# Low-rank k and q of four octets at a time on eight TensorE tiles, and experts by slots of two octets

## The chip, the cores and the metric

The kernel runs on one core of a Trainium2 chip. The metric is the device time of one execution in microseconds (us), lower is better. The engines are named as in the profile: PE (TensorE), with PEld its weight loads, DVE (VectorE), ACT (ScalarE), POOL (GpSimd), and SP (SyncE), whose queue issues all DMAs here.

## The reference

Two layers on x of 4 images, 64 channels, 256 x 256 pixels, float32. Both add their result to x and begin with a group norm (32 groups).

```
layer 0, per image, x the normalised input:
  h  = gelu(conv3x3(x, c1) + c1_b)
  xa, k = split(c2 * h + c2_b)                    # 64 + 64 channels, 1x1
  xs = gelu(conv over columns(conv over rows(xa)))  # 3 taps each, per channel
  weights = softmax(mean over pixels(xs) @ gate.T); the best two of three experts are kept
  out = xs + sum over experts e of  mask_e * w3_e (  (w2_e k + b2_e) * (w1_e xs + b1_e) )
  layer 0 = x_in + proj(out)
layer 1:
  h = relu(batchnorm(conv3x3(x, quantised w1)))
  h = batchnorm(conv3x3(h, quantised w2));   layer 1 = x_in + relu(h + x)
```

The three experts have 2, 4 and 8 ranks, 14 in all. The change is in the experts: `low = (w2 k + b2) * (w1 xs + b1)` has 14 (padded to 16) rows per pixel, and its product with w3 and proj is added to layer 0's result once the image's gate is known.

## The kernel before

An image is 128 pairs of rows. 128 partitions hold 64 channels of two rows; a *group* is 2 pairs (512 elements of a partition), an *octet* 4 pairs (8 rows), a *chunk* 8 pairs. Each image has 32 octets and 16 chunks.

A dictionary `plan` holds (step, order) for every call, and all calls are written out in that order (`at(step, order, call)`). In the first stage, the *front*, one step is one octet: 4 x 32 = 128 steps (`CONV1` = 128). For octet n of image b at step g = 32 b + n, PE's order in a step is

- order 1 and 7: `front_conv_a`, `front_conv_b` with products (1, 2) of octet n, the 3x3 convolution on 64x64 tiles into one of two PSUM banks `ps_c`; order 3 and 8 of the next step do products (0, 3);
- 7.5 and 8.5: `front_butterfly` (ACT and DVE) and `front_h`: two gelu activations that make h of one octet from its `ps_c` bank and so free it;
- step g + 3, order 4 and 9: `front_taps_a`, `front_taps_b` (`ps_a`, one bank), order 11 `front_taps_h`: t on ACT, two additions and the ends on DVE, then xs by gelu on ACT;
- step g + 4, order 6: `front_proj` (`ps_p`), added by DVE, stored to `t1_d`;
- order 2: the experts of image b - 1 (`out_octets`), order 3.5 the statistics of image b + 1;
- order 10: `front_k` and `front_q`, each for two octets j = 0 to 15: k at step 2j + 4, q at step 2j + 5.

Thus every step of the front has either a k or a q behind its last taps group. `front_v` (order 9 and 9.5) makes the convolution's inputs on POOL in `v_ring`. `divide` (order 5) puts a tiny POOL operation, the tick, between two uses of a bank.

`front_k` multiplies h with a weight `wk` whose other 64 rows are zero, on tiles of 128 rows by 32 columns: four groups of 512 to four strips of 32 partitions, ACT copies them to `k`. `front_q` does the same from xs, DVE adds a bias and multiplies by k into `low`, which goes to DRAM (`low_d`). Bank `p` (one buffer) is used by k, q, proj, the experts and all small matmuls in turn.

`plan_out` runs an image behind: `low_load` and `out_load` bring `ranks` and y back, `out_octets` makes two matmuls from 32 rows (`ps_o`) for one octet, and DVE adds each group to y (L746) and takes its statistics (L747). PE, SP, DVE and POOL keep the written order; ACT keeps it from step 124 on, and before that the scheduler orders it.

After step 128 the second stage (`conv1`, two steps per octet) runs layer 1's first convolution of all images, while the last octets of the front are done at half the pace (`tail`), and the experts of image 3 are spread over it. `leave` takes its result from PSUM: ACT makes `m`, DVE adds. `conv1_prepare` and `conv1_add` put sums of pixels in the buffers of t and xs. Then conv2 and a last stage follow, which the change doesn't touch in substance.

Of the kernel before, what the change touches and what calls it, by code (L numbers as in the profile page):

```python
# [17 lines left out]
B, C, H, W = 4, 64, 256, 256  # L18
P = 128


# [24 lines left out]
GP = 2  # L46
GF = GP * W
# [15 lines left out]
def conv_preact_kernel(ctx: ExitStack, tc: tile.TileContext, io, col128, colset, col64):  # L63
# [23 lines left out]

    low_d = [dram.tile([P, NG // 4, GF], F32, name=f"low_d{b}") for b in range(B)]
    y_d = [dram.tile([P, NPAIR, W], F32, name=f"y_d{b}") for b in range(B)]
# [99 lines left out]
    def weights():  # L189

        mset = flat(chunk_x("mset"))[:, 0 : io["mset"].shape[1]]
        m64_t = work.tile([P, 2, GF], F32, tag="xs", name="m64", bufs=3)
        m64 = flat(m64_t)[0:C, 0 : io["m64"].shape[1]]
# [129 lines left out]

    def leave(h, ps, ps_m, n, name, pool, tag, w, bias):

        m = pool.tile([P, 4 * HW], F32, tag=tag, name=f"m_{name}", bufs=2)[:, 0 : n * HW]
        nc.scalar.activation(m, by_two(ps_m)[:, 0, 0 : n * HW], AF.Identity, bias=bias, scale=w_scale[w])  # L327
        nc.vector.scalar_tensor_tensor(  # L328
            h.rearrange("p a (b e) -> p e (a b)", e=2),
            by_two(ps)[:, :, 0 : n * HW],  # L330
            w_scale[w],
            m.unsqueeze(1).to_broadcast([P, 2, n * HW]),
            ALU.mult,
            ALU.add,
        )
# [45 lines left out]
    def stats_group(b, g):  # L381
        if g == 0:
            st_x[b] = stat.tile([P, NG, 6], F32, tag="st_x", name=f"st_x{b}")
        t = x_in[b, g // CG]
        i = g % CG * GP
        nc.vector.bn_stats(st_x[b][:, g, :], t[:, i : i + GP, :])  # L386
# [216 lines left out]
    def front_taps_h(b, n):  # L603

        ps = open_a.pop((b, n)).rearrange("p a b c -> p (a b) c")
        t = work.tile([P, 2 * GP, W], F32, tag="t", name=f"t_{b}_{n}", bufs=1)
        nc.scalar.activation(flat(t), flat(ps), AF.Identity, bias=tap_bias, scale=sh[:, 1:2])  # L607
        nc.vector.scalar_tensor_tensor(  # L608
            t[:, :, 1:W], ps[:, :, 0 : W - 1], sh[:, 0:1], t[:, :, 1:W], ALU.mult, ALU.add
        )  # L610
        nc.vector.scalar_tensor_tensor(  # L611
            t[:, :, 0 : W - 1], ps[:, :, 1:W], sh[:, 2:3], t[:, :, 0 : W - 1], ALU.mult, ALU.add
        )
        nc.vector.tensor_tensor(  # L614
            t[:, :, 0 : W : W - 1],
            t[:, :, 0 : W : W - 1],
            ends.unsqueeze(1).to_broadcast([P, 2 * GP, 2]),
            ALU.subtract,
        )
        for at_n, slot, row in ((0, 0, 0), (NOCT - 1, 1, GP + 1)):  # L620
            if n == at_n:
                edge = t[0:C, row, :]
                nc.vector.tensor_tensor(edge, edge, outer[0:C, slot, :], ALU.subtract)
        xss[b, n] = work.tile([P, 2, GF], F32, tag="xs", name=f"xs_{b}_{n}", bufs=3)
        nc.scalar.activation(flat(xss[b, n]), flat(t), AF.Gelu, accum_out=pooled[b][:, n : n + 1])  # L625

    def front_k(b, j):

        ps = flat(bank("p", f"ps_k_{b}_{j}")[:, 0])
        for t in range(2):  # L630
            for q in range(4):
                nc.tensor.matmul(  # L632
                    ps[32 * q : 32 * q + 32],
                    wk[:, q % 2, t, :],
                    flat(hs[b, 2 * j + q // 2, t]),
                    start=(t == 0),
                    stop=(t == 1),
                )
        k_sb[b, j] = work.tile([P, GF], F32, tag="k", name=f"k_{b}_{j}")
        nc.scalar.activation(k_sb[b, j], ps, AF.Identity, bias=k_bias)  # L640

# [22 lines left out]
    def front_q(b, j):  # L664

        ps = flat(bank("p", f"ps_q_{b}_{j}")[:, 0])
        for q in range(4):
            x = xss[b, 2 * j + q // 2][:, q % 2]
            nc.tensor.matmul(ps[32 * q : 32 * q + 32], c128("e_w1"), x, start=True, stop=True)  # L669
        for n in (2 * j, 2 * j + 1):  # L670
            del xss[b, n]
        low = work.tile([P, GF], F32, tag="low", name=f"low_{b}_{j}")
        nc.vector.scalar_tensor_tensor(low, ps, c128("e_b1"), k_sb.pop((b, j)), ALU.add, ALU.mult)
        nc.sync.dma_start(low_d[b][:, j, :], low)
# [4 lines left out]
    def gate(b):  # L679
# [26 lines left out]
        for e, (i, j) in enumerate(((3, 4), (0, 5), (1, 2))):  # L706
# [3 lines left out]

        pick = stat.tile([P, 3, 3], F32, tag="pick", name=f"pick_{b}")
        of = c128("of").rearrange("p (i e) -> p i e", e=3)
        nc.vector.tensor_tensor(pick[:, 0:2, :], keep.unsqueeze(1).to_broadcast([P, 2, 3]), of, ALU.mult)
        nc.vector.tensor_tensor(pick[:, 2, :], keep, pb3, ALU.mult)
        row = stat.tile([P, 3], F32, tag="row", name=f"row_{b}")
        nc.vector.tensor_reduce(row, pick, AX.X, ALU.add)
        wm[b] = lstat.tile([P, 2, C], F32, tag="wm", name=f"wm_{b}", bufs=B)
        nc.vector.tensor_tensor(
            wm[b], row[:, 0:2].unsqueeze(2).to_broadcast([P, 2, C]), pw3.unsqueeze(1).to_broadcast([P, 2, C]), ALU.mult
        )  # L720
        out_bias[b] = stat.tile([P, 1], F32, tag="ob", name=f"ob_{b}", bufs=B)
        nc.vector.tensor_tensor(out_bias[b], row[:, 2:3], c128("proj_b"), ALU.add)

# [4 lines left out]
    def low_load(b, k):  # L728
        lows[b, k] = work.tile([P, GF], F32, tag="ranks", name=f"ranks_{b}_{k}", bufs=3)
        nc.sync.dma_start(lows[b, k], low_d[b][:, k, :])  # L730

    def out_octets(b, k, octets):


        if k == 0 and 0 in octets:
            st_y[b] = stat.tile([P, NG, 6], F32, tag="st_y", name=f"st_y{b}")
        ps = bank("p", f"ps_o_{b}_{k}_{octets[0]}")
        ranks = lows[b, k]
        for n, i in enumerate(octets):
            for g in range(2):  # L740
                rows = slice(64 * i + 32 * g, 64 * i + 32 * g + 32)
                nc.tensor.matmul(flat(ps[:, 2 * n + g]), flat(wm[b][rows]), ranks[rows], start=True, stop=True)  # L742
        for n, i in enumerate(octets):
            for g in range(2):
                y = ys[b, k][:, 4 * i + g : 4 * i + g + 3 : 2, :]
                nc.vector.scalar_tensor_tensor(y, ps[:, 2 * n + g], out_bias[b], y, ALU.add, ALU.add)  # L746
                nc.vector.bn_stats(st_y[b][:, 4 * k + 2 * i + g, :], y)  # L747
        if 1 in octets:
            y = ys.pop((b, k))
            del lows[b, k]  # L750
            for half in range(2):
                for g in range(2):
                    nc.sync.dma_start(
                        y_v[b][half, g][:, k * CG : (k + 1) * CG],
                        y[half * C : half * C + C, g::2],
                    )
# [30 lines left out]
    def conv1_add(b, k):  # L787
        sums_in[b, k] = add_pixels(y_in[b, k], f"1_{b}_{k}", [(work, "xs", 3)] * 2, [P, 2, GF])

    def conv1_prepare(b, k):  # L790

        places = (work, "t", 1), (work, "xs", 3)
        sums_in[b, k] = add_pixels(y_in[b, k], f"1_{b}_{k}", places, [P, 2, GF])
# [17 lines left out]
    def conv1_b(b, d):  # L811
# [12 lines left out]
        h = h_out[b][:, i : i + 2 * GP, :]  # L824
        leave(h, ps, ps_m, 2 * GP, f"1_{b}_{d}", work, "low", "w1", c128("b1"))
        for g in range(2):
# [9 lines left out]
    def conv1_end(b):  # L836
# [6 lines left out]
        convolve_sum(ps_m, "w1", sums[(NCH - 1) % 2], CPAIR, 1, (0,))  # L843
        leave(h, ps, ps_m, 1, f"1_{b}_end", work, "low", "w1", c128("b1"))
        nc.vector.bn_stats(st_h[b][C:P, NG, :], h[C:P, 0, :])
# [36 lines left out]
    def plan_front(b):  # L882
# [6 lines left out]
        for n in range(NOCT):  # L889
# [18 lines left out]
            at(place(g + 3), 11, front_taps_h, b, n)  # L908
        for j in range(NG // 4):
            at(place(t + 2 * j + 4), 10, front_k, b, j)  # L910
            at(place(t + 2 * j + 5), 10, front_q, b, j)
        e = place(t + NOCT + 3)
# [14 lines left out]
    def plan_out(b, steps, order, end):  # L927

        for k in range(NCH):
            for call in (low_load, out_load):  # L930
                at(steps[2 * k - 3] if k > 1 else steps[0] - 2, order + 0.2, call, b, k)
            for i in range(2):
                at(steps[2 * k + i], order, out_octets, b, k, (i,))
        at_each(end, out_end(b))
# [135 lines left out]
    def conv2_out(d, h, ps, ps_m):  # L1070
        b, k = chunks[d // 2]
        n = d % NOCT
        leave(h, ps, ps_m, 2 * GP, f"2_{d}", halves_pool, "m", "w2", c128("b2"))
        for g in range(2):
# [89 lines left out]
def _layout(a):  # L1164
# [43 lines left out]

    of = np.zeros((2, 2, 2, 2, 16, 3), f)
    for half, group in np.ndindex(2, 2):  # L1210
        of[half, :, group, half ^ group, np.arange(NLOW), expert] = 1.0
    chan = np.arange(P) % C
# [8 lines left out]
        "gate": twice(l0["gate_w"].T[:, [0, 1, 2, 0, 0, 1, 1, 2, 2]]),  # L1221
        "of": of.transpose(1, 2, 3, 4, 0, 5).reshape(P, 6),
        "sh": twice(l0["sh_w"].reshape(C, 3)),
# [37 lines left out]
```

## Time and profile before

| | us |
|---|---|
| median of 3 runs | 3368.22 (3367.95 to 3368.89) |
| profiled execution | 3364.82 |
| its span | 3363.0 |
| PE busy | 2730.7 (81%) |
| DVE busy | 2707.6 (81%) |
| ACT busy | 1668.5 (50%) |
| POOL busy | 1610.5 (48%) |
| front | about 68 to 1510 us |
| conv1 | about 1520 to 2270 us, with the experts of image 3 up to about 2070 |
| conv2, then the last stage | about 2285 to 2890 us, then to the end |

The span lies between the first and the last instruction of the profiled execution, its time contains a little more. "L441" is a line of the kernel; L441 records all quarter matmuls, so its groups are told apart by their tiles (`ps_c`, `ps_a`, `ps_p`). One fp32 matmul of the program is two MATMUL instructions in the profile. In an instruction row the idle time before it and its releaser stand in brackets.

### The profile page before, as it was taken

Reading aid. Unit: us, or ns where it says so; the run is one execution under the profiler, and the core shown is the slowest. Engines: PE = TensorE matmul, PEld = TensorE weight load, DVE = VectorE, ACT = ScalarE, POOL = GpSimd, SP = SyncE. Lnnn points to the kernel's source line nnn. Section 1 sums busy time; section 2 is a strip of 40 time slices with the busy share of each in tenths; the row PEclk is TensorE's granted clock in tenths of the full one; section 3 lists DMA queues with packets and bytes.
Section 4 is the critical chain, followed back from the end, with each engine's and each line's share of the span. In section 5 each row is a group of like instructions: output and inputs, shape, how many; then the busy total and the mean of one; then the engine's idle time right before and its main releaser. Section 6 shows DMA issues by size and latency. Waiting matters only on the chain.

```text
span 3363.0 us, 60903 instructions
## 1 busy us (share of the span) xinstructions
PE 2730.7 (81%) x24832; PEld 1758.7 (52%) x24832; DVE 2707.6 (81%) x2970; ACT 1668.5 (50%) x1831; POOL 1610.5 (48%) x1833
## 2 busy tenths in 40 slices
PE   2999999999999999997899999998999999300000
PEld 1555545555555555544667677777877878200000
DVE  7676588878888777775899998998999999866666
ACT  0344444344444443444556666767777777322222
POOL 2444544443444444444678777666777777100000
PEclk9999999999999999998999999999999999655555
DMA  8665688879887767774789887664666664599999
GB/s 299 171 184 131 160 262 267 249 199 275 259 262 208 212 192 199 209 202 139 244 276 298 300 286 239 222 249 182 238 232 237 239 239 165 207 412 412 412 412 389
DMA packets 365671, 838.28 MB, mean 249 GB/s; under 512 B 23312, under 2 KB 285968, under 8 KB 302672
## 3 DMA queue, kind: packets, MB, share of 16 engines
q1 hardware_dynamic: 365392, 834.40, 75.1%
q8 instruction: 195, 3.19, 0.4%
q14 instruction: 84, 0.69, 0.1%
HBM read 493.00 MB, written 341.31 MB: 248 GB/s over the span
## 4 chain that ended last, share of the span: by engine, by line
PE 71%; DVE 11%; DMA 11%; ACT 2%; SPq 2%; issue 2%; POOL 1%; ACTq 0%; DVEq 0%; POOLq 0%
PE ps_h L304 25%; PE ps_c L441 19%; DMA y_end<-y_d 10%; PE ps_a L441 9%; PE ps_h2m L304 3%; PE ps_k L632 3%; PE ps_o L742 3%; PE ps_p L441 3%; PE ps_hm L304 3%; PE ps_q L669 2%; DVE half L348 2%; DVE h L328 1%; DVE st_x L386 1%; SPq L1148 1%; ACT v L1139 1%
## 5 line engine op out<-in xcount | busy, mean ns | idle before, releaser
L304 PE MATMUL ps_h<-half,w_q 128*128 128x512 f32 x4096 | 1036.3, 405 | 28.6 <-DVE h L328 22.3
L304 PEld LDWEIGHTS ps_h<-half,w_q 128*128 128x128 f32 x4096 | 780.8, 192 | 260.4 <-issue 29.2
L484 POOL TENSOR_TENSOR v_ring<-x 128x256 f32<-128x256 f32 x1024 | 596.0, 614 | 157.4 <-PE ps_c L441 111.3
L364 POOL TENSOR_TENSOR sum<-s,sum 128x640 fp32r<-128x640 f32 (+1 forms) x256 | 556.6, 2194 | 193.8 <-ACT sum L362 188.2
L328 DVE SCALAR_TENSOR_TENSOR h<-ps_h,scale_w,m 128x1024 f32<-128x1024 f32 x256 | 326.9, 1277 | 92.6 <-ACT m L327 92.4
L441 PE MATMUL ps_c<-v_ring,u 64*64 64x256 f32 (+1 forms) x6472 | 389.2, 371 | 13.2 <-POOL v_ring L484 9.2
L441 PE MATMUL ps_c<-v_ring,c1s 64*64 64x256 f32 (+1 forms) x6472 | 386.1, 368 | 0.5 <-DVE ps_c L552 0.5
L441 PE MATMUL ps_a<-h,av 64*64 64x512 f32 (+1 forms) x3568 | 382.3, 530 | 1.7 <-DVE t L611 1.6
L441 PEld LDWEIGHTS ps_c<-v_ring,u 64*64 64x64 f32 x6472 | 254.0, 133 | 242.4 <-issue 77.5
L434 POOL MEMSET tick<- 128x1 f32 x132 | 13.0, 98 | 697.0 <-PE ps_a L441 686.8
L441 PEld LDWEIGHTS ps_c<-v_ring,c1s 64*64 64x64 f32 x6472 | 261.8, 133 | 134.4 <-issue 38.7
L550 ACT ACTIVATE m<-ps_c 128x512 f32<-128x512 f32 x128 | 76.6, 598 | 474.6 <-PE ps_c L441 467.6
L625 ACT ACTIVATE xs<-t 128x1024 f32<-128x1024 f32 x128 | 135.3, 1057 | 326.1 <-DVE t L614 293.5
L1139 ACT ACTIVATE v<-y_end,shift,gn 128x2048 f32<-128x2048 f32 x64 | 133.8, 2092 | 320.6 <-DMA y_end<-y_d 313.8
L1140 DVE SCALAR_TENSOR_TENSOR h<-h,ss,v 128x2048 f32<-128x2048 f32 x64 | 150.2, 2351 | 159.8 <-DMA h<-h_d 94.3
L348 DVE TENSOR_TENSOR half<-h,half 128x1280 fp32r<-128x1280 f32 (+1 forms) x128 | 254.4, 2029 | 7.7 <-ACT half L346 7.7
L656 DVE TENSOR_TENSOR x<-ps_p,x 128x1024 f32<-128x1024 f32 x128 | 156.3, 1221 | 121.2 <-PE ps_p L441 100.7
L608 DVE SCALAR_TENSOR_TENSOR t<-ps_a,m,t 128x1020 f32<-128x1020 f32 x128 | 163.6, 1278 | 93.8 <-ACT t L607 93.8
L441 PEld LDWEIGHTS ps_a<-h,av 64*64 64x64 f32 x3568 | 163.8, 133 | 113.0 <-issue 78.1
L327 ACT ACTIVATE m<-ps_hm,m,scale_w 128x512 f32<-128x512 f32 x128 | 99.4, 777 | 223.0 <-PE ps_hm L304 222.9
L348 DVE TENSOR_TENSOR half<-yn,half 128x1280 fp32r<-128x1280 f32 x80 | 201.9, 2540 | 4.2 <-ACT half L346 4.2
L746 DVE SCALAR_TENSOR_TENSOR y<-ps_o,ob,y 128x512 f32<-128x512 f32 x256 | 189.3, 740 | 17.1 <-PE ps_o L742 15.9
(186 smaller groups left out, 4203.4 us busy)
## 6 DMA issues: line engine op xcount, KB each, us to landing
h_d<-h SPq DMA_DIRECT2D x117, 1024.0 KB, 4.8
h<-h_d SPq DMA_DIRECT2D x64, 1152.0 KB, 7.1
yn<-y_d SPq DMA_DIRECT2D x60, 1152.0 KB, 7.7
xs_in<-in_x SPq DMA_DIRECT2D x64, 1024.0 KB, 8.8
x<-in_x SPq DMA_DIRECT2D x256, 256.0 KB, 4.9
y<-t_d SPq DMA_DIRECT2D x64, 1024.0 KB, 8.7
y_d<-y SPq DMA_DIRECT2D x256, 256.0 KB, 4.6
y_end<-y_d SPq DMA_DIRECT2D x64, 1024.0 KB, 11.2
```

Of the source, the lines that this page charges most:

```text
L304: nc.tensor.matmul(ps[:, 0 : n * HW], w[:, k, m, :], t[:, i + m : i + m + n, c : c + HW], start=(j == 0), stop=(j == len(terms) - 1),)
L328: nc.vector.scalar_tensor_tensor(h.rearrange("p a (b e) -> p e (a b)", e=2), by_two(ps)[:, :, 0 : n * HW], w_scale[w], m.unsqueeze(1).to_b ...
L348: engine.tensor_tensor(lower, y, upper.bitcast(F32), ALU.subtract)
L364: nc.gpsimd.tensor_tensor(tiles[1][:, a:e, :], t, tiles[0][:, a:e, :].bitcast(F32), ALU.subtract)
L441: last[:] = [nc.tensor.matmul(ps[o, at_out[0] : at_out[1], :], w[i], rhs[i], **flags)]
L484: nc.gpsimd.tensor_tensor(v_ring[:, o : o + 2, p, :], *terms[p])
L608: nc.vector.scalar_tensor_tensor(t[:, :, 1:W], ps[:, :, 0 : W - 1], sh[:, 0:1], t[:, :, 1:W], ALU.mult, ALU.add)
L625: nc.scalar.activation(flat(xss[b, n]), flat(t), AF.Gelu, accum_out=pooled[b][:, n : n + 1])
L656: nc.vector.tensor_tensor(t1, ps, t1, ALU.add)
L746: nc.vector.scalar_tensor_tensor(y, ps[:, 2 * n + g], out_bias[b], y, ALU.add, ALU.add)
L1139: nc.scalar.activation(v, y, AF.Identity, bias=shift[:, b : b + 1], scale=gn2[b][:, 1:2])
L1140: nc.vector.scalar_tensor_tensor(h, h, ss2[:, 0:1], v, ALU.mult, ALU.add)
```

## The change

k and q are made for four octets at a time, j = 0 to 7. k of a group of rows comes from the 64 partitions that hold it, with a 64x32 weight: four octets give four strips of 32 partitions, and the two halves of the partitions go to two PSUM banks, eight tiles in all. q keeps its 128x32 tiles, with two rounds of four strips. ACT's and DVE's instructions on them have 1024 elements instead of 512. `low` overwrites k in its tile, of which there is one.

k moves from order 10 of step 2j + 4 to order 0.5 of step 4j + 5, q from order 10 of step 2j + 5 to order 10 of step 4j + 7. Stores and loads of low have 512 KB, one for two chunks. The experts (`out_slot`) take one slot of two octets: two matmuls from 32 rows as before, one addition of 1024 elements, two statistics of 512; the expert weights `wm` have four columns of 64 rather than two. xs gets four buffers instead of three, ranks two larger ones instead of three. `leave` in conv1 takes its m from the buffers of ranks (first four octets of image 0) or of k (one buffer), where it had two of low; `conv1_prepare` for k = 2 takes ranks for one sum.

```diff
-        ps = flat(bank("p", f"ps_k_{b}_{j}")[:, 0])
+        ps = bank("p", f"ps_k_{b}_{j}").rearrange("p s a b -> p s (a b)")
         for t in range(2):
-            for q in range(4):
-                nc.tensor.matmul(
-                    ps[32 * q : 32 * q + 32],
-                    wk[:, q % 2, t, :],
-                    flat(hs[b, 2 * j + q // 2, t]),
-                    start=(t == 0),
-                    stop=(t == 1),
-                )
-        k_sb[b, j] = work.tile([P, GF], F32, tag="k", name=f"k_{b}_{j}")
-        nc.scalar.activation(k_sb[b, j], ps, AF.Identity, bias=k_bias)
+            for i in range(4):
+                for s in range(2):
+                    half = slice(s * C, s * C + C)
+                    nc.tensor.matmul(
+                        ps[32 * i : 32 * i + 32, s],
+                        wk[half, s, t, :],
+                        flat(hs[b, 4 * j + i, t])[half],
+                        start=(t == 0),
+                        stop=(t == 1),
+                    )
+        k_sb[b, j] = work.tile([P, 2, GF], F32, tag="k", name=f"k_{b}_{j}", bufs=1)
+        nc.scalar.activation(flat(k_sb[b, j]), ps.rearrange("p s f -> p (s f)"), AF.Identity, bias=k_bias)
...
-        ps = flat(bank("p", f"ps_q_{b}_{j}")[:, 0])
-        for q in range(4):
-            x = xss[b, 2 * j + q // 2][:, q % 2]
-            nc.tensor.matmul(ps[32 * q : 32 * q + 32], c128("e_w1"), x, start=True, stop=True)
...
+        ps = bank("p", f"ps_q_{b}_{j}").rearrange("p s a b -> p s (a b)")
+        for s in range(2):
+            for i in range(4):
+                x = xss[b, 4 * j + i][:, s]
+                nc.tensor.matmul(ps[32 * i : 32 * i + 32, s], c128("e_w1"), x, start=True, stop=True)
...
+        low = flat(k_sb.pop((b, j)))
+        nc.vector.scalar_tensor_tensor(low, ps.rearrange("p s f -> p (s f)"), c128("e_b1"), low, ALU.add, ALU.mult)
         nc.sync.dma_start(low_d[b][:, j, :], low)
...
+        if k % 2 == 0:
+            lows[b, k // 2] = work.tile([P, 2, GF], F32, tag="ranks", name=f"ranks_{b}_{k}", bufs=2)
+            nc.sync.dma_start(flat(lows[b, k // 2]), low_d[b][:, k // 2, :])
...
-    def out_octets(b, k, octets):
+    def out_slot(b, k, s):
...
+        ps = bank("p", f"ps_o_{b}_{k}_{s}")
+        for i in range(2):
+            rows = slice(32 * (2 * k % 4 + i), 32 * (2 * k % 4 + i) + 32)
+            nc.tensor.matmul(
+                flat(ps[:, i]),
+                flat(wm[b][rows, 2 * s : 2 * s + 2, :]),
+                lows[b, k // 2][rows, s],
+                start=True,
+                stop=True,
+            )
+        y = ys[b, k][:, s::2, :]
+        nc.vector.scalar_tensor_tensor(y, ps.rearrange("p i a b -> p (i a) b"), out_bias[b], y, ALU.add, ALU.add)
+        for i in range(2):
+            nc.vector.bn_stats(st_y[b][:, 4 * k + 2 * s + i, :], y[:, 2 * i : 2 * i + 2])
...
-        places = (work, "t", 1), (work, "xs", 3)
+        places = (work, "t", 1), ((work, "ranks", 2) if k == 2 else (work, "xs", 4))
...
-        leave(h, ps, ps_m, 2 * GP, f"1_{b}_{d}", work, "low", "w1", c128("b1"))
+        place = (work, "ranks", 2, [P, 2, GF]) if b == 0 and d < 4 else (work, "k", 1, [P, 2, GF])
+        leave(h, ps, ps_m, 2 * GP, f"1_{b}_{d}", place, "w1", c128("b1"))
...
-        for j in range(NG // 4):
-            at(place(t + 2 * j + 4), 10, front_k, b, j)
-            at(place(t + 2 * j + 5), 10, front_q, b, j)
+        for j in range(NOCT // 4):
+            at(place(t + 4 * j + 5), 0.5, front_k, b, j)
+            at(place(t + 4 * j + 7), 10, front_q, b, j)
```

## The prediction

> **What bounds the kernel now.** I read the page first: the slices of the span and its chain. TensorE (PE) is the largest share of that chain and is full in the first half, where the change lies. The windows by stage say how full: in 430 to 780 us PE is busy 346.4 of 350 us.
>
> ```profile
> PE 71%; DVE 11%; DMA 11%; ACT 2%; SPq 2%; issue 2%; POOL 1%; ACTq 0%; DVEq 0%; POOLq 0%
> ...
> 430.00:780.00 350.00, 346.41 (x4639) 179.75 (x4643) 294.20 (x404) 140.55 (x200) 152.10 (x296) 1.00 0.84 244
> ```
>
> The second row's columns are window and length, then busy us of PE, weight loads, VectorE (DVE), ScalarE (ACT) and GpSimd (POOL), then clock, DMA share and GB/s. DVE is at 84%, so it has room. Next the timeline of two steps of the front, an ordinary pair:
>
> ```profile
> 620.24 1.96 PE L441 MATMUL ps_c<-v_ring,u 64*64 64x256 f32 x32
> ...
> 629.27 1.04 PE L441 MATMUL ps_a<-h,av 64*64 64x512 f32 x8
> ...
> 629.58 1.39 ACT L558 ACTIVATE h<-ps_c,c1b 128x512 f32<-128x512 f32 x2 [0.33 <-PE ps_c L441]
> ...
> 630.24 1.92 PE L632 MATMUL ps_k<-h,wk 128*32 128x512 f32 x16
> ...
> 632.10 1.96 PE L441 MATMUL ps_c<-v_ring,u 64*64 64x256 f32 x32
> ...
> 642.09 1.06 PE L669 MATMUL ps_q<-xs,m 128*32 128x512 f32 x8
> ...
> 643.09 0.44 PE L441 MATMUL ps_c<-v_ring,u 64*64 64x256 f32 x3
> ```
>
> Each row gives start, length, engine, line, tiles. A step runs from one first conv group (`ps_c<-v_ring,u`, front_conv_a) to the next: 11.86 us with a k in it, 10.99 with a q, in turn, without a PE gap. The stretch that matters I call the boundary: from the start of the last taps group (`ps_a` x8) to the next conv_a. It is 632.10 - 629.27 = 2.83 us with k and 1.97 with q (the same at nearly every step). It holds 0.86 of taps, 0.11 of entry, then 1.86 of k or 1.00 of q. Two rounds of four matmuls are 0.86 us (taps), so k is four rounds (1.72) and 0.14 of exit.
>
> What lies under the boundary? conv_a of octet n takes the `ps_c` bank that h of octet n-2 (front_h, two activations) empties. Those end at 629.58 + 1.39 = 630.97, 1.70 after the boundary began. Today k or q covers that. Step 3 of the first image, which has neither, shows it uncovered:
>
> ```profile
> 98.97 1.04 PE L441 MATMUL ps_a<-h,av 64*64 64x512 f32 x8
> ...
> 99.30 1.33 ACT L558 ACTIVATE h<-ps_c,c1b 128x512 f32<-128x512 f32 x2 [0.27 <-PE ps_c L441]
> ...
> 100.73 1.96 PE L441 MATMUL ps_c<-v_ring,u 64*64 64x256 f32 x32 [0.72 <-POOL v_ring L484]
> ```
>
> PE stands for 0.72 us. The row names POOL, but v_ring was done long before; h ended at 100.63. An empty boundary is thus 1.76 us, only 0.21 less than one with q.
>
> **What the Trainium skill says.** "TensorEngine Tiling (Array Packing)", Tiling Modes, lists 64x32 as eight tiles and says under Key Properties that a change of mode drains the array. The trace agrees with the drain (0.11 in, 0.14 out at k) and shows no eight-tile group; four tiles start within 20 ns of each other and the next four 0.43 us later. Its Gotcha 1 (PSUM Pressure) says that different row tiles must write different PSUM banks; the change puts its two row halves in two banks, and the conv (64x64) does so today. "TensorE: Matmul & The Clock Gate", What's actually happening, says that an idle window of about 3.4 us halves the clock. The trace agrees: the q after a wait of 5.67 us (1536.2) takes 1.93 us, not 1.06.
>
> **The change, part by part**, per four octets of the front.
>
> *k on PE.* Before two groups of 16 instructions at 1.86; after one of 32 on eight tiles. If eight run at once that is again four rounds, 1.86 with exit. It moves from the end of steps 2j+4 to the start of step 4j+5, and now needs the newest h, of octet 4j+3. The tiles of the first three octets start at once; the fourth waits for the first h activation, which ends about 1.10 after the boundary's start, with its semaphore about 1.15, against a k start at 0.97: +0.2. Boundary 2.83 + 0.2 = 3.03.
>
> *q on PE.* Before two groups of two rounds, after one of four: boundary 0.97 + 1.72 + 0.14 = 2.83, once.
>
> *The two boundaries left without either*: 1.76 each, set by h.
>
> Sum: before 2 x (2.83 + 1.97) = 9.60; after 3.03 + 2.83 + 2 x 1.76 = 9.38. Gain 0.2 per four octets, times 31 = **-6 us**. The group times alone promise far more: 2 x (0.11 + 1.86) + 2 x (0.11 + 1.00) = 6.16 becomes 2 x 1.97 = 3.94, so 2.2 x 31 = 69 us. The difference is the cover that k and q gave: h is what is late next.
>
> *Small matmuls.* Statistics and out_end issue one at order 9.9 or 9.95; the view shows k at 3.50 and q at 2.60 there, +0.65. Eight of these (two for each of three images' statistics, two of out_end) fall in boundaries that become empty, where they run under the wait for h: 8 x 0.65 = **-5 us**.
>
> *PSUM bank p.* It is single, and passes k, o (out_slot), proj, q. k's eviction grows from 0.69 to about 1.1 us (xs, 128x1024, is 1.06) and follows t in ACT's order in all but two cases; it ends about 4.2 after the boundary's start, and o comes at 3.03 + 1.89 = 4.92: covered by 0.7. At step 125 ACT's order is fixed by hand from step 124 on, and puts k's eviction behind xs of the octet before: bank free at about 8.1, o waits: **+3 us**, once.
>
> *q's eviction* is one of 1.28 (as L608) where there were two of 0.75. It delays taps_h by 1.3 in one step of four; L611 then ends at 6.8 and taps_a comes at 7.6, so it is hidden by 0.8.
>
> *One k buffer.* low lies in k's tile, and the next k eviction waits for its store, twice as large (512 KB). q's eviction ends at 4.2; k's next could start at about 15. The 256 KB store lands in 7.4 us at the median and 9.4 at most; t_d's of 512 KB 8.2 and 10.4. With the SP issue (1.4) it lands by 13 to 15: just hidden. SP stands 1.4 us longer before that store, with x and y loads behind it; they are one to three steps ahead. Stores and loads of low become 32 each.
>
> *o.* PE's work is unchanged (4 instructions, 1.06). DVE has one addition of about 1.27 (x<-ps_p of the same size is 1.22) for two of 0.735: -0.2 x 128 = -26 us of DVE, hidden in the front. In conv1, where 36 of them lie and DVE releases ps_h in short stretches, I take **-2 us** (0 to -7).
>
> *conv1 and the tail.* The m of leave gets one buffer; it waits for the addition of d-1, and the two bn_stats (1.29) between two additions cover its 0.78. In the tail q(j=14) and k(j=15) go, which waited for x<-ps_p (5.67 and 3.19) and ran at half clock (1.93 and 3.46). But the chain there runs through ACT, POOL and t's one buffer, and m of d=2 now shares a slot with a sum that POOL frees about 5 us later: I get -1 to +1. q(j=6) with its longer eviction stands before L608: **+1.5**. The 4th xs buffer only holds four octets for q.
>
> Sum: -6 - 5 + 3 - 2 + 1.5 = -8.5. The profiled execution took 3364.8 (span 3363.0); the median of the runs is 3368.2, 3.4 above. So 3368.2 - 8.5, about **3359.5**.
>
> **Bounds of what the trace does not show.** Eight tiles: from four rounds (taken: 64x64 already pairs rows and banks, 128x32 already has four columns) to eight rounds, +1.72 x 32 = +55. The drain into 64x32: 0.25 (as 128x32) to none, -8. An empty boundary: 1.70 to 1.85, -4 to +6.
>
> **Rivals.**
> 1. *k's buffer decides* (slower). If the low store lands over 11 us after q's eviction, k's eviction holds bank p and o waits, us for us, in the 24 groups that have an o, with ACT's queue (xs) behind it. For: one buffer, DMA at 84 to 100% in these slices. Against: 9.4 at most so far. At 1.0 us each: +24, 3383.5 on my sum (at 1.3, 3390); it turns the sign from about 0.4 us each.
> 2. *Eight tiles don't run at once* (slower): +55, 3414. Against: both halves of the form run today.
> 3. *The h wait isn't there*: PE gains its group times in full: -69 for -6, 3297. Against: the 0.72 gap at 100.73.
> 4. *The transition costs more*: m in one slot with the sums, k behind xs: +10 on my sum, 3369. This lands on no change.
>
> **Numbers.** Main case 0.60, with its own range 3342 to 3372 (down to all favourable bounds: drain -8, boundary -4, conv1 -5; up to boundary +6 and some of rival 4); rival 1 0.17; rival 2 0.05; rival 3 0.03; rival 4 0.15. No change means within 0.2% (6.7 us), about what a measurement of this kernel can tell. Of the main case 0.41 is below 3361.5, 0.16 within, 0.03 above; rival 3 adds 0.03 to faster; rival 4 gives 0.08 to no change and 0.07 to slower; rival 1 0.01 to no change and 0.16 to slower; rival 2 0.05 to slower. Faster 0.44, same 0.25, slower 0.31. The range 3342 to 3390 takes in rivals 1 and 4 and leaves out 2, 3 and the ends.
>
> **What would show it.** Right: 32 k groups of 32 instructions at about 1.9 to 2.1 us; boundaries of 3.0, 1.76, 1.76, 2.8 in turn; ps_c waiting for h in half of the steps; PE busy time down by some 60 to 70 us while the front is only about 10 shorter. Wrong: k groups of 3.5 us (rival 2); ps_o waiting for ACT's k each fourth step, with k waiting for the low store (rival 1); boundaries under 1.5 us (rival 3).

## The result and the profile after

The changed kernel takes 3359.5 us (median of 13 runs, 3357.12 to 3363.29), beside 3366.9 us for the kernel before in the same session; the ratio is 0.998, 95% interval 0.9972 to 0.9989. It is 7 us faster, close to what can be told from no change, and the forecast was 3359.5. That the two agree to the tenth is luck: the forecast was -8.5 from a median of 3368.2 in three runs, the measured change is -7.4 from 3366.9. The number also came out for the wrong reason, as the experiments show: the terms of the sum that I put on k and q add up to nothing that can be told, and nearly all of the 7 us comes from the one addition of the experts, to which I gave 2.

First the page after, the shares of the chain. PE's share fell from 71 to 67%, and "issue", waits that the profile can't name, rose.

```profile
PE 67%; DVE 11%; DMA 11%; issue 3%; ACT 2%; POOL 2%; SPq 2%; ACTq 0%; POOLq 0%; DVEq 0%
```

The window of the second image (columns as before: PE, weight loads, DVE, ACT, POOL, clock, DMA share, GB/s): PE is busy 338.5 of 350 us where it was 346.4. PE has less to do, but the kernel isn't faster by as much: part of the time PE stands idle.

```profile
430.00:780.00 350.00, 338.49 (x4688) 185.11 (x4688) 288.84 (x370) 140.25 (x196) 154.20 (x298) 1.00 0.82 246
```

The timeline of four octets after, with the rows that carry the boundaries (from the last `ps_a` x8 to the next `ps_c<-v_ring,u`):

```profile
923.41 1.03 PE L444 MATMUL ps_a<-h,av 64*64 64x512 f32 x8
...
923.68 1.33 ACT L561 ACTIVATE h<-ps_c,c1b 128x512 f32<-128x512 f32 x2 [0.26 <-PE ps_c L444]
...
925.11 1.96 PE L444 MATMUL ps_c<-v_ring,u 64*64 64x256 f32 x32 [0.67 <-POOL v_ring L487]
...
934.14 1.04 PE L444 MATMUL ps_a<-h,av 64*64 64x512 f32 x8
...
935.91 1.96 PE L444 MATMUL ps_c<-v_ring,u 64*64 64x256 f32 x32 [0.73 <-POOL v_ring L487]
...
944.94 1.04 PE L444 MATMUL ps_a<-h,av 64*64 64x512 f32 x8
...
945.91 1.92 PE L676 MATMUL ps_q<-xs,m 128*32 128x512 f32 x16
...
947.77 1.96 PE L444 MATMUL ps_c<-v_ring,u 64*64 64x256 f32 x32
...
956.79 1.03 PE L444 MATMUL ps_a<-h,av 64*64 64x512 f32 x8
...
957.76 2.01 PE L638 MATMUL ps_k<-h,wk 64*32 64x512 f32 x32
...
959.70 1.96 PE L444 MATMUL ps_c<-v_ring,u 64*64 64x256 f32 x32
```

Two boundaries hold neither k nor q: 925.11 - 923.41 = 1.70 and 1.77 us, with PE idle for 0.67 and 0.73 until h (from 923.68, 1.33 long) has emptied `ps_c`. The one with q is 2.83, the one with k 2.91. The medians over the front are 1.74, 2.83 and 2.95. In the list of PE's waits between 110 and 1480 us (total, times, longest) this has become the first entry; before it was 2.1 us, 3 times:

```profile
PE ps_c L444 <- POOL v_ring L487: 34.8, 50, 0.7
PE ps_c L444 <- issue: 4.4, 10, 0.7
```

Both rows are that wait for h: in all 60 places the conv group starts 0.10 us after the end of an h (0.098 to 0.100), while the operation on `v_ring` that the first row names had ended 0.7 us before, at the median.

### The profile page after: what moved, and what is told of

It is laid out like the page before. It is cut to its first block, busy times and chain, and to the rows that moved or that the text cites. A ratio compares the mean times of both kernels' runs of the same rounds, so it can differ in the third digit from the quotient of the medians.

```text
span 3357.7 us, 60548 instructions
## 1 busy us (share of the span) xinstructions
PE 2682.6 (80%) x24832; PEld 1776.4 (53%) x24832; DVE 2680.4 (80%) x2810; ACT 1659.6 (49%) x1799; POOL 1610.8 (48%) x1833
## 4 chain that ended last, share of the span: by engine, by line
PE 67%; DVE 11%; DMA 11%; issue 3%; ACT 2%; POOL 2%; SPq 2%; ACTq 0%; POOLq 0%; DVEq 0%
PE ps_h L305 24%; PE ps_c L444 19%; DMA y_end<-y_d 10%; PE ps_a L444 8%; PE ps_o L749 3%; PE ps_h2m L305 3%; PE ps_p L444 3%; PE ps_hm L305 2%; DVE half L351 2%; PE ps_k L638 2%; PE ps_q L676 2%; DVE h L331 2%; POOL v_ring L487 1%; DVE st_x L389 1%; SPq L1163 1%
## 5 line engine op out<-in xcount | busy, mean ns | idle before, releaser
L444 PEld LDWEIGHTS ps_c<-v_ring,u 64*64 64x64 f32 x6472 | 266.4, 134 | 266.5 <-POOL v_ring L487 142.5
L611 DVE SCALAR_TENSOR_TENSOR t<-ps_a,m,t 128x1020 f32<-128x1020 f32 x128 | 163.5, 1278 | 122.8 <-ACT t L610 122.8
L351 DVE TENSOR_TENSOR half<-yn,half 128x1280 fp32r<-128x1280 f32 x80 | 210.4, 2646 | 4.2 <-ACT half L349 4.2
L561 ACT ACTIVATE h<-ps_c,c1b 128x512 f32<-128x512 f32 x256 | 174.1, 739 | 38.8 <-PE ps_c L444 38.8
```

The lines of the kernel that those rows point to most:

```text
L351: engine.tensor_tensor(lower, y, upper.bitcast(F32), ALU.subtract)
L444: last[:] = [nc.tensor.matmul(ps[o, at_out[0] : at_out[1], :], w[i], rhs[i], **flags)]
L561: nc.scalar.activation(h.rearrange("p q (c e) -> p e q c", e=2), c[:, t].rearrange("p (e q c) -> p e q c", e=2, q=GP), AF.Gelu, bias=c1_bi ...
L611: nc.vector.scalar_tensor_tensor(t[:, :, 1:W], ps[:, :, 0 : W - 1], sh[:, 0:1], t[:, :, 1:W], ALU.mult, ALU.add)
```

## The experiments

The start of the program, before the front is under way, differs by chance: octet 4 starts its conv at 97.9 us in the first trace after and between 99.5 and 102.4 in the traces of the experiments. Where I compare traces I count from there. Edits are to the changed kernel, except in the last two parts.

### Is it the wait for h?

o, 1.06 us of PE, goes ahead of the first conv group in the two of four steps with an empty boundary. Nothing is added or taken away.

```diff
-                at(steps[2 * k + i], order, out_slot, b, k, i)
+                s = steps[2 * k + i]
+                early = s < CONV1 and s % 4 in (2, 3)
+                at(s, 0.7 if early else order, out_slot, b, k, i)
```

> The experts' matmuls (o, 1.06 us of PE) go ahead of the first conv group in the two of four steps whose boundary holds neither k nor q; nothing else moves. Theory (PE stands there for the h that frees ps_c): the boundary holds 0.97 of taps, 1.06 of o and the entry, so it is about 2.05 long for 1.74, but the 1.06 of o is gone from the step: -0.75 each, in 2 of 4 steps of images 1 to 3 where an o lies, about 46 boundaries: -34 us, about 3326. Rival A (the boundary is not a wait for h but time that PE needs itself, or a wait for v_ring as the row says): o only changes its place, 0 +- 3 us, 3359. Rival B (DVE, at 83% there, or the single bank p, whose o is now emptied before the proj of the step, is next): half of it, 3340 to 3350, with ps_a waiting for DVE L614 more often.

3330.6 us, ratio to before 0.9896 (0.9879 to 0.9913): 29 us faster than the changed kernel. In its timeline o stands where PE stood:

```profile
916.57 1.03 PE L444 MATMUL ps_a<-h,av 64*64 64x512 f32 x8
...
916.84 1.35 ACT L561 ACTIVATE h<-ps_c,c1b 128x512 f32<-128x512 f32 x2 [0.25 <-PE ps_c L444]
...
917.53 1.13 PE L749 MATMUL ps_o<-ranks,wm 32*128 32x512 f32 x4
...
918.59 1.96 PE L444 MATMUL ps_c<-v_ring,u 64*64 64x256 f32 x32
```

The boundary is 2.02 us for 1.74 and the step is rid of 1.06. By the medians of the four steps, 45.37 us become 43.78. Rival A is refuted: PE doesn't need that time itself, by this run, and it doesn't wait for `v_ring`, by the 0.10 us above (o would have covered that wait too, so this run alone couldn't tell). Of rival B there is no sign in the ordinary steps: they gain 1.6 us per four, a little more than the 1.5 expected, and `ps_a` waits for DVE L614 7 times, 2.9 us in all, as without the edit. The part of the 34 us that didn't come is missing in a few steps around the statistics and the gates. The same h after the same conv releases the bank as before: what was missing was work to put over it.

### Is it the eight tiles?

```diff
-                        wk[half, s, t, :],
-                        flat(hs[b, 4 * j + i, t])[half],
+                        wk[:, s, t, :],
+                        flat(hs[b, 4 * j + i, t]),
```

> k of four octets as in the change, but from all 128 rows with the zero-padded weights on 128x32 tiles, as the kernel before had them: same instructions, evictions, transfers, places. If eight 64x32 tiles do run at once and that is what pays for taking k and q together, a k group takes eight rounds: 2.04 becomes about 3.7 us and the boundary about 4.7; 32 groups by 1.7 are +55 us, about 3414, which is 47 above the kernel before. Rival: 128-row tiles hide behind the wait for the newest h (0.2 us) or the rounds overlap, then +48 at most; if the saving came from joining alone, it stays at 3360.

3412.2 us, ratio 1.0143 (1.0122 to 1.0163), 53 us above the changed kernel. The row of a k group in its timeline:

```profile
946.00 3.75 PE L638 MATMUL ps_k<-h,wk 128*32 128x512 f32 x32
```

The same 32 instructions take about 3.75 us on tiles of 128 rows and 1.95 to 2.12 on tiles of 64. Eight tiles run at once, and taking four octets together does nothing for k by itself. Without the 64x32 form this schedule is 46 us slower than the kernel before, so the form for the most part pays back what the empty boundaries cost.

### k behind xs at step 125

k of octets 24 to 27 of image 3 is written inside `front_taps_h` of the step before, between t and xs.

```diff
         nc.scalar.activation(flat(t), flat(ps), AF.Identity, bias=tap_bias, scale=sh[:, 1:2])
+        if (b, n) == (B - 1, NOCT - 7):
+            front_k(b, NOCT // 4 - 2)
...
-            at(place(t + 4 * j + 5), 0.5, front_k, b, j)
+            if (b, j) != (B - 1, NOCT // 4 - 2):
+                at(place(t + 4 * j + 5), 0.5, front_k, b, j)
```

> One k group alone (image 3, octets 24 to 27) is written between t and xs of the step before, so that ACT, whose order is fixed there, empties k's bank ahead of xs. The changed kernel lost 5.2 us in that step: o waited 3.0 us for k's bank, and then ran at half the clock. If that order is the cause, the step goes from 16.7 to about 11.6 us and the time falls by 4 to 5 us, 3354 to 3356 where the changed kernel has 3359.5. Rival: the bank is late for another reason (the step lies at the change to conv1), or the gain is lost again behind it at the start of conv1; then the step is shorter but the end not, 3359.

The rows after, then those of this experiment:

```profile
1468.35 1.06 ACT L628 ACTIVATE xs<-t 128x1024 f32<-128x1024 f32 x1 [2.93 <-DVE t L617]
...
1469.40 1.09 ACT L646 ACTIVATE k<-ps_k,k_bias 128x1024 f32<-128x1024 f32 x1
...
1470.55 2.08 PE L749 MATMUL ps_o<-ranks,wm 32*128 32x512 f32 x4 [3.00 <-ACT k L646]
...
1472.56 3.69 PE L444 MATMUL ps_c<-v_ring,c1s 64*64 64x256 f32 x32
```

```profile
1470.88 1.12 ACT L648 ACTIVATE k<-ps_k,k_bias 128x1024 f32<-128x1024 f32 x1 [0.31 <-PE ps_k L640]
...
1472.64 1.13 PE L751 MATMUL ps_o<-ranks,wm 32*128 32x512 f32 x4
...
1473.49 1.06 ACT L630 ACTIVATE xs<-t 128x1024 f32<-128x1024 f32 x1 [1.50 <-DVE t L619]
```

After, o waits 3.00 us for the bank, and because PE stood so long, o takes 2.08 for 1.13 and the next conv group 3.69 for 1.96. With k's eviction first the step is 10.73 us long for 16.73. The time is 3354.3 us (0.9967, 0.9955 to 0.9979), 5 below the changed kernel. Its profiled execution was the longest of its nine, 3360.5: there conv1's first `ps_h` comes 2.9 us sooner than in the second trace of the changed kernel (`r_after`, below), but the end 0.6 us later, so the rival's loss happens in some executions.

### q's eviction ahead of the taps in image 0

```diff
-            at(place(t + 4 * j + 7), 10, front_q, b, j)
+            at(place(t + 4 * j + 7), 11.2 if b == 0 else 10, front_q, b, j)
```

> In image 0 alone (which has no experts) q stands behind taps_h in the written order, so that DVE does its eviction of 1.28 us behind the additions L611 and L614 of the octet and no longer ahead of them. The changed kernel loses 0.6 us per four octets in image 0 where I had a gain of 0.2. If that eviction is the cause (ps_a waits 0.41 for L614), image 0 gets 0.3 to 0.8 per four octets back, 3 to 6 us over 8 groups, and the time is 3354 to 3357. Rival: the loss sits in the h wait of the empty boundaries, which in image 0 come sooner for want of an o; then nothing changes, or proj waits for bank p, which now comes free later: 3359 to 3362.

3361.5 us (0.9987, 0.9981 to 0.9993), no better than the changed kernel, and yet the trace shows the cause that was expected. Seven times the step after q is 10.76 us for 11.38 at the median, together 4.2 us. The eighth q meets the gate of image 0 and its first o, and there its eviction comes last:

```profile
441.40 1.27 DVE L680 SCALAR_TENSOR_TENSOR k<-ps_q,m,k 128x1024 f32<-128x1024 f32 x1
...
442.73 2.08 PE L749 MATMUL ps_o<-ranks,wm 32*128 32x512 f32 x4 [4.71 <-DVE k L680]
```

o waits 4.71 us for bank p, with PE at half speed behind it: 20.0 us for a step of 13.0 in the first trace after, which takes the gain back and more.

### The edits together

e7 holds o in the empty boundaries, k ahead of xs, and q behind the taps in image 0 but for its last four octets.

> Three edits on the changed kernel together: the one k group ahead of xs (-5.2 alone), o in the empty boundaries (-29 alone), and q behind taps_h in image 0 but for its last four octets (in the run with all eight, seven groups gained 0.63 each and the last lost 7, where o and the gate lie). If the three are independent: -5 -29 -4.4 from 3359.5, 3321. If a gain is lost again where the front meets conv1, or waits overlap: 3324 to 3328.

3320.7 us, ratio 0.986 (0.9847 to 0.9874): the gains of the three add up, as far as this can tell.

e8 also moves half of image 0's proj groups to the next step, ahead of its first conv group:

```diff
-            at(place(g + 4), 6, front_proj, b, n)
+            early = b == 0 and n % 4 in (1, 2) and n < NOCT - 3
+            at(*((g + 5, 0.7) if early else (place(g + 4), 6)), front_proj, b, n)
```

> As the three edits together, and in image 0, which has no experts to fill the empty boundaries, half of the proj groups (1.03 us) go a step later, ahead of the first conv group there. If PE stands there for h as in the other images, 13 boundaries give 0.75 each: -10, about 3311. Rival: in image 0 it is DVE (ps_a waits for L614) that is next, so that less than half comes: 3317 to 3321; or the later proj holds the x chunk and the t1 store longer and loads come late: no gain or a loss.

3315.5 us, ratio 0.9847 (0.9833 to 0.986), the best version of the study, but half of what I expected. The boundary is 1.75 us with proj as without, so proj is free there. The step is shorter by 0.28 and not by 0.86, since proj had covered something in its old place too: PE now waits for POOL's tick.

```profile
238.78 1.09 PE L444 MATMUL ps_c<-v_ring,u 64*64 64x256 f32 x20 [0.33 <-POOL tick L437]
```

### What is the one addition worth?

The additions of the changed kernel taken apart:

```diff
-        nc.vector.scalar_tensor_tensor(y, ps.rearrange("p i a b -> p (i a) b"), out_bias[b], y, ALU.add, ALU.add)
         for i in range(2):
+            part = y[:, 2 * i : 2 * i + 2]
+            nc.vector.scalar_tensor_tensor(part, ps[:, i], out_bias[b], part, ALU.add, ALU.add)
             nc.vector.bn_stats(st_y[b][:, 4 * k + 2 * s + i, :], y[:, 2 * i : 2 * i + 2])
```

> The changed kernel with the experts' one addition of 1024 elements taken apart into two of 512, each before its statistics, as the kernel before had them. DVE gets 27 us more (128 times 2 x 0.735 for 1.27). Theory: hidden in the front, where PE is the bound, 0 to 1 us there; in conv1, where DVE releases ps_h, 1 to 3 us; together 3360 to 3363. Rival: DVE at 83% is near enough to a bound that a good part counts, 10 to 25 us, 3370 to 3385; then the addition was what made the change faster at all.

3367.6 us (1.0004, 0.9996 to 1.0013): 8 us more, and no different from the kernel before. That was neither of the two cases. So the addition went alone into the kernel before, with k and q as they were, and the pair of changed kernels ran again on one chip:

> The kernel before, k and q as they were, with the experts alone changed: a slot of two octets, two matmuls and one addition of 1024 elements for two of 512. Taking the addition apart in the changed kernel cost 8.1 us by the medians, though its trace shows only 2.7 of it behind the start. If the addition is worth 8 us by itself, this kernel takes 3358 to 3360, as the changed one, and k and q by four octets are worth nothing in sum (the prediction had -2 for the addition, -6.5 for the rest). If it is worth what the trace of the undone one shows, 3363 to 3365, and k and q bring the other 4. Rival: before, where the boundaries are full of k and q, DVE is off the path and it brings nothing, 3366; then the addition pays only together with the new order.

> The changed kernel once more, beside the next one on one chip: 3359 to 3361 if its first 13 runs stand. The time of its third conv step (97.9 us in its first trace, 100 to 102 in those of four kernels with the same instructions up to there) shows whether 4 us of start are chance: then it is elsewhere in this trace.

> The changed kernel with two additions of 512 once more, beside it: 3366 to 3369 if the 8 us stand and belong to the additions; 3361 to 3364 if most of it was the start or the chip. From the third conv step on its trace is 2 to 5 us longer than that of the changed kernel, in the steps where an image's gate meets the experts.

| kernel | us | ratio to before |
|---|---|---|
| before, one addition | 3356.8 | 0.9971 (0.996 to 0.9983) |
| changed | 3359.0 | 0.9975 (0.9967 to 0.9983) |
| changed, two additions | 3366.0 | 0.9998 (0.999 to 1.0007) |

The addition alone gives the whole gain; k and q by four octets give none that these runs can tell. The traces show one place where it comes from. This is a step of `r_two_adds` behind a gate:

```profile
1191.23 0.74 DVE L759 SCALAR_TENSOR_TENSOR y<-ps_o,ob,y 128x512 f32<-128x512 f32 x1
...
1192.00 0.70 DVE L760 BATCH_NORM_STATS2 st_y<-y 128x6 f32<-128x512 f32 x1
...
1192.61 0.73 DVE L759 SCALAR_TENSOR_TENSOR y<-ps_o,ob,y 128x512 f32<-128x512 f32 x1
...
1193.38 0.69 DVE L760 BATCH_NORM_STATS2 st_y<-y 128x6 f32<-128x512 f32 x1
...
1193.49 1.09 PE L444 MATMUL ps_p<-xs,m 64*64 64x512 f32 x8 [0.56 <-DVE y L759]
```

and the same step of `r_after`:

```profile
1188.44 1.27 DVE L757 SCALAR_TENSOR_TENSOR y<-ps_o,ob,y 128x1024 f32<-128x1024 f32 x1
...
1189.75 1.29 DVE L759 BATCH_NORM_STATS2 st_y<-y 128x6 f32<-128x512 f32 x2
...
1189.97 1.03 PE L444 MATMUL ps_p<-xs,m 64*64 64x512 f32 x8
```

proj needs bank p. With two additions the bank is free only behind the second, and a statistic stands between them: 2.1 us after the first began, for 1.27. Where the gate's chain (the small DVE instructions that compute it) has made DVE late, proj waits for it. But DVE itself is also done sooner, 2.60 us after the first addition began for 2.84.

### DVE's time or the bank?

The kernel before with its own two additions, both ahead of the two statistics: the same instructions in another order.

```diff
                 nc.vector.scalar_tensor_tensor(y, ps[:, 2 * n + g], out_bias[b], y, ALU.add, ALU.add)
+            for g in range(2):
+                y = ys[b, k][:, 4 * i + g : 4 * i + g + 3 : 2, :]
                 nc.vector.bn_stats(st_y[b][:, 4 * k + 2 * i + g, :], y)
```

> The kernel before with its own two additions of 512, but both ahead of the two statistics, where addition and statistics took turns. DVE works as long as before (0.735 x 2 + 0.70 x 2); bank p comes free 0.7 us sooner behind each o. If one addition helped because proj waits for bank p behind the second addition in the steps where an image's gate makes DVE late (the traces show 0.8 less there, three times, and 0.25 in other steps), this gives most of it: 0.6 to 0.8 for 0.9, 3 us in the front, and 3358 to 3362 if the medians of the one addition (-10) come from the bank. If it is the 0.2 us of DVE time for each slot that counts (conv1), it stays at 3366 to 3367.

> The kernel before with one addition once more: its profiled execution was the longest of its seven, 6 us above their median, and its trace explains 3.9 us in the front and gives 2 of them back later. If the other 6 are in the kernel, 3356 to 3359 again, and a trace of that length shows them in conv1 (from the end of the front to the first combine of the batch norm 2 to 5 us shorter than 2269.7 us less its front). If they were the chip's, 3361 to 3364.

Adds first: 3357.6 us, 0.9975 (0.9967 to 0.9984). One addition again: 3358.4 us, 0.998 (0.9971 to 0.9989). An order of four instructions gives what the addition gives, and what the whole change gives. The step above, in the kernel with the additions first:

```profile
1188.37 1.40 DVE L746 SCALAR_TENSOR_TENSOR y<-ps_o,ob,y 128x512 f32<-128x512 f32 x2
...
1189.69 1.27 DVE L749 BATCH_NORM_STATS2 st_y<-y 128x6 f32<-128x512 f32 x2
...
1189.91 1.09 PE L441 MATMUL ps_p<-xs,m 64*64 64x512 f32 x8
```

proj runs without a wait. But the run doesn't separate the bank from DVE's time as I had expected. The two additions take 1.40 us in a row and the two statistics 1.27, less than when they take turns, and DVE is done 2.59 us after it began, as soon as with one addition:

| medians of the 128 slots, us from the first addition's start | bank p free | DVE done |
|---|---|---|
| before | 2.13 | 2.86 |
| additions first | 1.41 | 2.60 |
| one addition | 1.28 | 2.60 |

The front does separate them in part. It is shorter by 3.7 us (additions first) and 3.9 (one addition) by the traces, in the same steps. The three steps behind the gates (36, 68, 100) gain 0.71 to 0.73 with additions first and 0.79 to 0.80 with one addition, close to the 0.72 and 0.85 by which the bank is free sooner: that is the bank, over half of the front's gain. Steps 67, 69, 70 and 83 gain 0.23 to 0.26 and step 125 gains 0.52, alike in both kernels. That fits DVE's 0.26, once or twice, but no run shows it.

Of the rest, some 5 to 6 us of the medians, the traces put 3.5 to 6.7 into conv1 in the three executions of the altered kernel before, nearly all of it between 1660 and 2119 us, where the experts of image 3 run; but between the changed kernel and its two-addition form the difference of 4.0 us is already there at the end of the front. I couldn't name the wait in conv1 that goes. DVE's 0.26 us for each of the 32 slots there isn't excluded, nor is PE's clock at the start of conv1, which is halved in some executions and not in others (last section). That part stays open.

## Why the prediction came out

Shifts against the kernel before in us, counted from octet 4's conv, at the starts of some steps and at the end of the profiled execution:

| | step 34 | 38 | 66 | 70 | 98 | 102 | 125 | 126 | conv1's first `ps_h` | end |
|---|---|---|---|---|---|---|---|---|---|---|
| changed, two additions (k and q alone) | +3.3 | +5.4 | +2.2 | +3.5 | +0.2 | +0.7 | -1.4 | +2.5 | +6.7 | -0.7 |
| changed (`r_after`) | +3.3 | +4.9 | +1.3 | +1.7 | -2.5 | -2.8 | -5.2 | -1.3 | +2.6 | -4.7 |
| before, one addition (`r_one_add`) | +0.1 | -0.7 | -0.7 | -2.0 | -2.6 | -3.4 | -3.4 | -3.9 | -4.1 | -8.8 |

**k and q on PE: right.** k is four rounds, its boundary 2.95 us for the 3.03 forecast; q 2.83; the empty ones 1.74 for 1.76. With experts the four steps are 0.33 us shorter (forecast 0.2). The statement that the group times alone promise 69 us and that h takes them is what the experiment with o confirms. With the small matmuls, image 1 gained 3.2, image 2 3.3 (first row, 38 to 66 and 70 to 98), in sum about as forecast for these images.

**Times 31: wrong.** I took the step of the experts for all. Image 0 has no o, so taps_a comes 1.06 us earlier, and the 0.8 by which I called q's eviction hidden is gone. It loses 0.7 per four octets (41.73 us for 41.06 by the medians) where I had a gain: +3.3 at step 34. The step that failed is "L611 then ends at 6.8 and taps_a comes at 7.6", read in a step with an o.

**The gates: missed.** The steps where an image's gate stands (34 to 38, and so on) cost +2.1, +1.3 and +0.5. q of the last four octets lies behind the chain of small DVE instructions, longer by its 1.28 us eviction, and o waits for it, 4.0 us in three places for 2.8 before. PE's clock is another part. Before, it is never halved at a gate. In both traces of the changed kernel it is halved for 3.4 us at the gates of images 0 and 1, behind several shorter waits. proj at the gate of image 0, before and in `r_after`:

```profile
430.27 1.09 PE L441 MATMUL ps_p<-xs,m 64*64 64x512 f32 x8 [1.27 <-DVE lg L690]
```

```profile
433.55 1.98 PE L444 MATMUL ps_p<-xs,m 64*64 64x512 f32 x8 [1.56 <-DVE lg L697]
```

At image 2's gate it is halved in the trace of the experiment with k before xs, and not in `r_after`, whose program is the same up to there: steps 98 to 102 are 1.7 us longer in the first.

**Step 125: right in cause, short in size.** +3 was the wait itself. The step lost 5.2 us in the first trace after and 3.9 in `r_after`, because behind the wait of 3.00 us (3.5 for the weight loads, by the list of waits) PE runs at half speed for o and the conv group. For this the forecast had nothing. The Trainium skill's "TensorE: Matmul & The Clock Gate", What's actually happening, which I had cited for q's 1.93, gives about 3.4 us of idleness; here a PE wait below that figure was enough.

**The transition: a little better than forecast, and not as I worked it out.** From the start of step 126 to the last proj of the tail the first two rows gain 1.5 and 1.8 us (forecast -1 to +1, and +1.5 for q). But conv1's first matmul comes later by 4 than the end of step 125 did, as the wait for v_ring in the tail is 5.6 to 5.8 us for 3.77 and PE then runs at half speed; by the last proj of the tail, from which q and k groups have gone, it is made up (+1.0 and -3.1 in the first two rows).

**The addition: near in DVE time, wrong in what it does.** DVE's busy time is 20.6 us lower with one addition (`r_after` beside `r_two_adds`; 22.3 in the kernel before), forecast 26. I saw that much time of an engine off the path and put -2 on it, in conv1. In the front, where I put it at nothing, what counts at the gates is when bank p comes free. It was in the list of waits before, 1.7 us in three places, and I didn't follow it:

```profile
PE ps_p L441 <- DVE y L746: 1.7, 3, 0.6
```

So the sum of -8.5 held by luck: -6.5 for k, q and the transition was 5 to 8 too good, and -2 for the addition 5 to 9 too small.

**The rivals.** k's one buffer never decided: the 512 KB store lands in 7.3 us at the median, as the 256 KB store before (7.4; 8.9 at most, the 9.4 of the forecast is a load), and k's eviction waits for no DMA. Eight tiles do run at once. The wait for h is there. From the start of step 125 to conv1's first `ps_h` the first two rows lose 8.1 and 7.8 us, not far from the 10 of rival 4, and the tail gives most of it back. PE's busy time fell by 48 us, less than the 60 to 70 forecast; between 90 and 1530 us its clock is halved for 24 us in the first trace after and never before, which by itself can make up to some 12 us of busy time.

## What to carry to other kernels

A group of matmuls that is joined or made faster leaves a hole where it stood: look which wait it covered, and put other work of the same engine there (here 1 us of o moved by one place gave 29 us, four times the whole change). A cost read in one step holds only where that step has the same neighbours; image 0 without its experts and the steps with a gate each had another answer. Before a shorter instruction on an engine off the path is priced at nothing, ask which buffer its end releases: one addition for two, or only both additions ahead of the statistics, released a shared PSUM bank 0.7 to 0.9 us sooner. And an experiment that only changes an order can still change how long an engine takes: look in its trace before calling the work the same.

## What I had not expected of the hardware

- Eight 64x32 tiles: 32 fp32 instructions of 512 columns in 1.95 to 2.12 us with exit, against about 3.75 on four 128x32 tiles. The eight tiles that the Trainium skill lists in "TensorEngine Tiling (Array Packing)", Tiling Modes, are shown here.
- The halving of PE's clock isn't settled by the length of one wait near the idle time that the Trainium skill gives in "TensorE: Matmul & The Clock Gate", What's actually happening (about 3.4 us). The same kernel, before with one addition, had it after a wait of 3.58 us in one execution and not after 3.59 in another; the stretch up to the next taps wait took 19.0 us for 14.5. At the gate of image 0 waits of 0.41 and 1.56 us a little apart were enough (`r_after`). The rows, first of `b1_one_add`, then of `r_one_add`:

```profile
1497.08 3.69 PE L441 MATMUL ps_c<-v_ring,u 64*64 64x256 f32 x32 [3.58 <-POOL v_ring L484]
```

```profile
1495.85 1.96 PE L441 MATMUL ps_c<-v_ring,u 64*64 64x256 f32 x32 [3.59 <-POOL v_ring L484]
```

- Two additions in a row and then two statistics take DVE 2.60 us, and 2.86 when each addition is followed by its statistic, with the same four instructions (medians of 128 slots).
- Four matmuls of proj, in the same tile form as the taps ahead of them, took 0.86 us in a boundary with no entry or exit cost; k and q, in another form, paid 0.25.
